# One unit earlier for x: loading, normalising and turning an x tile in three successive units, and eight products of zeros at the start

## The chip, the cores and the metric

The kernel runs on one core of a Trainium2 chip. The metric is the device time of one execution in microseconds (us). TensorE is called PE, VectorE DVE, ScalarE ACT, GpSimd POOL, SyncE SP. All transfers of this part of the kernel are issued on SP's queue, in the order of the program.

## The reference

A cross-attention layer and a feed-forward layer with a shared and sixteen routed experts, on x of 32 sequences by 100 tokens by 512. All is f32.

```
x = x + xattn(layernorm(x), ctx, ctx, WQ, WK, WV, Wfc, bfc)
      # 16 heads of 32; q = ln(x) WQ^T, k = ctx WK^T, v = ctx WV^T, causal softmax(q k^T / sqrt(32)) v
x = x + ffn(layernorm(x))
      # shared gated FFN over all tokens, and 16 experts that each take their 12 best tokens of a sequence
```

With the causal mask only the first 100 rows of a context are ever attended to. The change touches only the first layernorm, the one ahead of q, and the start of the program.

## The kernel before, in words

**Products.** A product that needs f32 accuracy is made of three: each operand is split into a high part (rounded to fp32r by a copy on ACT) and a low part (the rest, a subtraction on DVE or POOL). `mm3` (L55) issues the three for each of four slices of 128. Plain f32 products are used where operands are small: the scores, the values and all turns.

**Stages.** The attention works on 8 super-blocks of 4 sequences (400 tokens), numbered sb. A super-block has 4 units, one for each group of 4 heads, c = 0 to 3; u = 4 sb + c counts the 32 units. Around them:

- A *prologue* loads and splits WK, WV and WQ, projects the first blocks of the context to keys (kproj, L55, kept by kkeep, L200, and stored to kD, L201) and values (vproj, vkeep), and makes the four x tiles of super-block 0.
- A *unit* u computes the scores of unit u-1 (L236 into the tile sc), its row maximum (sm_max, L247, 16 instructions on DVE), subtracts it (sm_sub, L256, POOL), takes the exponential (sm_exp, L260, ACT), the row sum (sm_sum, L265, DVE) and multiplies with its reciprocal (sm_mul, L271, POOL), each in two halves. For unit u-2 it turns the four probability tiles (p_turn, L277, kept on ACT by p_keep, L282) and multiplies them with the values (values, L292, kept a unit later by y_keep, L299). It projects the query of unit u (qproj, qkeep L226) and, in the units up to 28, a piece of a later block of the context: always a kproj, and a vproj except where ck reaches the block's number of 128-row pieces, which is so in all units with c = 0 from unit 4 on.
- *x tiles.* An x tile is one sequence, 100 by 512. x_load (L145) fetches it, x_stats (L152, L153 on DVE, L154, L155 on POOL) takes mean and 1/sqrt(var), x_norm (L161, DVE, in place) normalises, x_turn (L167) turns its four slices on PE and splits the result into xnh (ACT, L100) and xnl (DVE, L101). In unit u the tile number c of super-block sb+1 has its statistics, its norm and its turn, all in this unit; its load is issued at the start of the unit before.
- The *feed-forward* part follows. It is not touched.

**Order.** The order on each engine is written out by hand (`manual_schedule`): every engine takes its instructions in program order, so the place of a call in the unit is its place in each queue that it uses. Within a unit the calls that matter here stand so:

```
kload, ctx_load, x_load | scores, y_keep, sm_max/sm_sub x2, qproj/qkeep, sm_exp(0)
p_turn(0,1), p_keep | x_stats | sm_exp(1), sm_sum(0), sm_mul(0) | kproj/kkeep
p_turn(2,3), p_keep | x_norm | sm_sum(1), sm_mul(1) | ctx_split | vproj/vkeep | x_turn | values
```

In units 9 to 12 a piece of Wfc is split as well (fc_split, L573 and L574), and unit 13 loads and prepares constants of the feed-forward part (load_consts, L563 to L569).

**Buffers.** The accumulators in PSUM are few: two tiles of `kv` (shared by kproj, vproj and qproj), two of `ms` (p_turn, values, x_turn) and one of `sc`. An instruction that writes a tile waits until the one before in that tile has been emptied. x has 5 buffers.

## Time and profile before

| | us |
|---|---|
| median of 3 runs | 1734.94 (1734.51 to 1736.95) |
| the profiled execution | 1736.99, of which the span of instructions is 1735.2 |
| PE busy | 1698.0 |
| DVE / ACT / POOL busy | 900.6 / 692.2 / 442.3 |
| prologue | 0 to about 41 |
| units | about 41 to 385 |
| feed-forward | the rest |
| one unit with a vproj, without | about 10.7, about 9.8 |

A row of the profile's timeline gives start, duration, engine, line, operation, the tiles written and read, and the count of instructions merged in the row; in brackets stands how long the engine was idle before it and what released it. A row of the list of waits gives who waited for whom, the sum, the number of times and the longest. A row of the table by windows gives the stretch, its length, the busy time of PE, of PE's weight loads, DVE, ACT and POOL with the number of instructions, then PE's granted clock (1.00 is full), the DMA engines' share and GB/s.

### The profile page before, as it was taken

The numbers are of one execution on the slowest core, as the hardware profiler recorded it, in microseconds if no ns is written. First come the engines' busy times: TensorE is split into PE (matmuls) and PEld (weight loads), VectorE is DVE, ScalarE is ACT, GpSimd is POOL, SyncE is SP. The second block draws the span as 40 slices with busy tenths as digits, with TensorE's granted clock in tenths as the row PEclk, the third lists the DMA queues.
The fourth block names the chain that finished last, engine by engine and source line by source line (L and its number), as shares of the span: only waits on it lengthen the run. The fifth ranks groups of instructions, "written<-read, shape, count | busy, mean of one in ns | idle before, by whom it ended". The sixth has DMA issues, their size and how long they took to land.

```text
span 1735.2 us, 28064 instructions
## 1 busy us (share of the span) xinstructions
PE 1698.0 (98%) x11072; PEld 1559.9 (90%) x11072; DVE 900.6 (52%) x2126; ACT 692.2 (40%) x1094; POOL 442.3 (25%) x399
## 2 busy tenths in 40 slices
PE   7999999989999999999999999999999999999999
PEld 6888888878899999998899999999999999999998
DVE  4877777785333433344654444544444454444442
ACT  4555555544221111122344444444444444444442
POOL 3777777661110110210111111111111111111011
PEclk9999999989999999999999999999999999999999
DMA  6445443434210211130445554555554554554452
GB/s 203 147 138 152 137 132 118 134 109 159 91 62 13 73 61 52 59 110 31 156 159 153 154 155 147 155 154 146 164 151 144 161 156 136 164 164 119 137 170 61
DMA packets 86836, 220.58 MB, mean 127 GB/s; under 512 B 9745, under 2 KB 38146, under 8 KB 86704
## 3 DMA queue, kind: packets, MB, share of 16 engines
q1 hardware_dynamic: 75632, 193.30, 34.1%
q0 software_dynamic: 10784, 25.21, 7.8%
q8 instruction: 87, 1.43, 0.4%
q14 instruction: 45, 0.37, 0.1%
q10 hardware_dynamic: 288, 0.27, 0.0%
HBM read 171.57 MB, written 47.18 MB: 126 GB/s over the span
## 4 chain that ended last, share of the span: by engine, by line
PE 93%; DVE 2%; POOL 2%; DMA 1%; ACT 1%; issue 1%; SPq 0%; ACTq 0%; POOLq 0%; DVEq 0%
PE gu L55 47%; PE dn L55 23%; PE kv L55 10%; PE m L55 4%; PE ms L277 2%; PE sc L236 2%; PE ms L292 2%; POOL p L256 1%; PE m L803 1%; DVE p L247 1%; DVE xt L161 1%; PE ms L167 1%; DMA kD<-kk 1%; PE m L918 1%; PE m L909 1%
## 5 line engine op out<-in xcount | busy, mean ns | idle before, releaser
L55 PE MATMUL gu<-xh,whl 128*128 128x384 f32 (+1 forms) x3200 | 645.1, 333 | 1.3 <-ACT g L655 1.3
L55 PEld LDWEIGHTS gu<-xh,whl 128*128 128x128 f32 x3200 | 558.9, 188 | 18.7 <-ACT g L655 1.5
L628 DVE TENSOR_TENSOR whl<-wraw,whl 128x1536 fp32r<-128x1536 f32 (+1 forms) x146 | 256.1, 1754 | 253.5 <-ACT whl L627 253.4
L55 PE MATMUL dn<-whl,hh 128*128 128x512 f32 x1168 | 372.2, 400 | 0.0
L55 PE MATMUL gu<-xl,whl 128*128 128x384 f32 (+1 forms) x1600 | 338.1, 333 | 0.0
L55 PEld LDWEIGHTS gu<-xl,whl 128*128 128x128 f32 x1600 | 280.6, 188 | 0.0
L659 ACT CAST hh<-g 128x384 fp32r<-128x384 f32 (+1 forms) x200 | 100.9, 505 | 431.5 <-DVE g L656 431.5
L656 DVE TENSOR_TENSOR g<-g,gu 128x384 f32<-128x384 f32 (+1 forms) x200 | 108.7, 543 | 295.5 <-PE gu L55 294.5
L627 ACT CAST whl<-wraw 128x1536 fp32r<-128x1536 f32 (+1 forms) x146 | 213.2, 1460 | 109.9 <-PE dn L55 108.9
L55 PEld LDWEIGHTS dn<-whl,hh 128*128 128x128 f32 x1168 | 213.0, 189 | 37.2
L55 PE MATMUL dn<-whl,hl 128*128 128x512 f32 x584 | 230.9, 395 | 0.0
L655 ACT ACTIVATE g<-gu 128x384 f32<-128x384 f32 (+1 forms) x200 | 96.8, 484 | 294.8 <-PE gu L55 294.7
L817 POOL DMA_INDIRECT out_dram<-x,isl x48 | 77.7, 1619 | 368.2 <-ACT x L816 358.4
L660 DVE TENSOR_TENSOR hl<-g,hh 128x384 fp32r<-128x384 f32 (+1 forms) x200 | 112.1, 560 | 114.3 <-ACT hh L659 114.3
L792 POOL DMA_INDIRECT big<-xnD,isl x48 | 49.2, 1025 | 412.3 <-PE m L803 345.6
L55 PEld LDWEIGHTS dn<-whl,hl 128*128 128x128 f32 x584 | 109.8, 188 | 26.1
L271 POOL TENSOR_TENSOR p<-p,sm 100x800 f32<-100x800 f32 x64 | 101.3, 1583 | 52.3 <-DVE sm L266 39.6
L256 POOL TENSOR_TENSOR p<-p,mx 100x800 f32<-100x800 f32 x64 | 96.5, 1529 | 49.4 <-DVE mx L247 49.4
L247 DVE CUSTOM_DVE_ANT_0 p<-sc,mask 100x100 f32<-100x100 f32 x512 | 95.6, 257 | 17.4 <-PE sc L236 17.4
L861 POOL TENSOR_TENSOR x<-x,bfc 128x512 f32<-128x512 f32 x22 | 38.7, 1786 | 185.0 <-DMA x<-x 185.0
L265 DVE TENSOR_REDUCE sm<-p 100x8 f32<-100x800 f32 x64 | 62.7, 979 | 13.4 <-ACT p L260 13.3
L260 ACT ACTIVATE p<-p 100x800 f32<-100x800 f32 x64 | 56.2, 878 | 17.5 <-POOL p L256 17.5
(143 smaller groups left out, 1655.3 us busy)
## 6 DMA issues: line engine op xcount, KB each, us to landing
wraw<-wE SPq DMA_DIRECT2D x144, 768.0 KB, 4.4
xt<-x SPq DMA_DIRECT2D x32, 200.0 KB
vD<-vt SPq DMA_DIRECT2D x25, 256.0 KB, 2.0
kt<-kD SPq DMA_DIRECT2D x32, 200.0 KB, 4.5
v<-vD SPq DMA_DIRECT2D x8, 800.0 KB
xnD<-xn SPq DMA_DIRECT2D x25, 256.0 KB, 2.0
out_dram<-x SPq DMA_DIRECT2D x25, 256.0 KB, 2.0
yD<-y SPq DMA_DIRECT2D x31, 200.0 KB, 4.4
```

The lines of the kernel that those rows point to most:

```text
L55: r = nc.tensor.matmul(out, t[0][a], t[1][b], start=(first and i == 0), stop=(last and i == n - 1))
L247: nc.vector.tensor_tensor_reduce(out=p[:, bb, h, :], in0=sc[:, h, cs], in1=mask, scale=ISCALE, scalar=NEG, op0=ALU.add, op1=ALU.max, accum ...
L256: nc.gpsimd.tensor_tensor(pv, pv, mx[:, :, None].to_broadcast([S, 8, S]), ALU.subtract)
L265: nc.vector.tensor_reduce(sm, pv, AX.X, ALU.add)
L271: nc.gpsimd.tensor_tensor(pv, pv, sm[:, :, None].to_broadcast([S, 8, S]), ALU.mult)
L627: nc.scalar.copy(h[:, cs], r[:, cs])
L628: nc.vector.tensor_tensor(l[:, cs], r[:, cs], f32(h[:, cs]), ALU.subtract)
L655: nc.scalar.activation(g[:, 0:t], pg[:, 0:t], AF.Gelu)
L656: nc.vector.tensor_tensor(g[:, 0:t], g[:, 0:t], pu[:, 0:t], ALU.mult)
L659: nc.scalar.copy(hh[:, 0:t], g[:, 0:t])
L660: nc.vector.tensor_tensor(hl[:, 0:t], g[:, 0:t], f32(hh[:, 0:t]), ALU.subtract)
L817: ins = nc.gpsimd.indirect_dma_start(out=self.K.out, out_offset=bass.IndirectOffsetOnAxis(ap=r.isl[:, i:i + 1], axis=0), in_=o, in_offset= ...
```

## The change

Three things are done.

1. The unit that turns tile (sb+1, c) no longer takes its statistics and its norm: unit u takes those of the tile that unit u+1 turns, and loads the one after that. The prologue takes over the first load, statistics and norm. x_norm stands behind sm_mul(1) now instead of ahead of sm_sum(1). The tiles xnh and xnl are taken at x_turn instead of at x_load.
2. Where a unit has no vproj, x_turn writes to a `kv` tile instead of an `ms` tile.
3. At the start of the prologue, PE multiplies a tile of zeros with itself eight times (128 by 128, f32), into an `ms` tile that nobody reads.

```diff
+WARM = 8
         def x_load(sb, b):
-            if b == 0:
-                cur["xh", sb] = xnp[sb % 2].tile([128, NC4, SB], FR, name="xnh")
-                cur["xl", sb] = xnp[sb % 2].tile([128, NC4, SB], FR, name="xnl")
             xt = xp.tile([S, D], F32, name="xt")
...
-        def x_turn(sb, b):
+        def x_turn(sb, b, own=True):
+            if b == 0:
+                cur["xh", sb] = xnp[sb % 2].tile([128, NC4, SB], FR, name="xnh")
+                cur["xl", sb] = xnp[sb % 2].tile([128, NC4, SB], FR, name="xnl")
             xt = cur["x", sb, b]
-            tp = ps_ms.tile([128, NC4, 128], F32, name="ms")
+            if own:
+                tp = ps_ms.tile([128, NC4, 128], F32, name="ms")
+            else:
+                tp = ps_kv.tile([128, D], F32, name="kv").rearrange("p (c t) -> p c t", c=NC4)
...
             nc.gpsimd.dma_start(mask, K.mask)
+            z = stp.tile([128, 128], F32, name="zero")
+            nc.vector.memset(z, 0.0)
+            zp = ps_ms.tile([128, NC4, 128], F32, name="ms")
+            for _ in range(WARM):
+                nc.tensor.matmul(zp[:, 0, :], z, z, start=True, stop=True)
...
+            x_load(1, 1)
             ctx_load(3, 0)
+            x_stats(1, 0)
             vkeep(1, 0, vproj(1, 0))
+            x_norm(1, 0)
...
+                xn = divmod(u + 5, NC4) if u + 5 < NU else None
...
-                    sn, bn = divmod(u + 5, NC4)
+                    sn, bn = divmod(u + 6, NC4)
                     if sn < nsb:
                         x_load(sn, bn)
...
-                if xs:
-                    x_stats(sb + 1, c)
+                if xn:
+                    x_stats(*xn)
...
-                if xs:
-                    x_norm(sb + 1, c)
                 if a is not None:
                     sm_sum(a, 1)
                     sm_mul(a, 1)
+                if xn:
+                    x_norm(*xn)
...
                 if xs:
-                    x_turn(sb + 1, c)
+                    x_turn(sb + 1, c, vv)
```

## The prediction

> **What bounds the kernel now.** I read the shares of busy time first, then the list of who waited for whom, then single units in the timeline, then TensorE's busy time and granted clock in windows.

> ```profile
> PE 1698.0 (98%) x11072; PEld 1559.9 (90%) x11072; DVE 900.6 (52%) x2126; ACT 692.2 (40%) x1094; POOL 442.3 (25%) x399
> ```

> TensorE (PE) is busy 98% of 1735.2 us, so 37 us are idle, and little but those can be won. "Busy" however says nothing of the clock at which it is busy. The list of waits tells who holds the idle time:

> ```profile
> PE ms L167 <- DVE xt L161: 10.4, 7, 1.7
> PE kv L55 <- ACT cxh L134: 4.9, 1, 4.9
> PE ms L277 <- ACT pt L282: 4.1, 3, 2.2
> ```

> The largest entry is x_turn (L167) waiting for x_norm (L161): 10.4 us in 7 waits. There are 28 such turns in the units; only 7 wait. Six of them are in units 4, 8, 12, 16, 20, 24, where no vproj stands between the last p_turn and x_turn (1.64 to 1.67 each), and one in unit 1 (0.46). Unit 4, in the timelines of the four engines:

> ```profile
> 78.79 0.85 PE L277 MATMUL ms<-ident,p 100*100 100x100 f32 x8
> 81.28 0.54 PE L167 MATMUL ms<-ident,xt 100*128 100x100 f32 x4 [1.64 <-DVE xt L161]
> 81.74 0.89 PE L292 MATMUL ms<-pt,v 100*32 100x100 f32 x32
> 79.38 1.75 DVE L161 TENSOR_SCALAR xt<-xt,mv,rs 100x512 f32<-100x512 f32 x1 [0.20 <-POOL rs L155]
> 79.33 1.52 POOL L271 TENSOR_TENSOR p<-p,sm 100x800 f32<-100x800 f32 x1
> 79.72 0.91 ACT L282 COPY pt<-ms 100x400 f32<-100x400 f32 x2
> ```

> x_norm takes 1.75 us here, 0.50 where POOL is idle (fastest of its 32): it runs beside sm_mul on POOL. From p_turn to values (L292) go 81.74-78.79 = 2.95 us. Unit 28 is the same unit with no x tile in it:

> ```profile
> 338.50 0.85 PE L277 MATMUL ms<-ident,p 100*100 100x100 f32 x8
> 339.99 0.89 PE L292 MATMUL ms<-pt,v 100*32 100x100 f32 x32 [0.64 <-ACT pt L282]
> ```

> There it is 1.49 us, set by ACT's copies of pt. That is the floor for the other six.

> The clock shows a second cost. Each row is a stretch of 3.4 us: busy times by engine, granted clock:

> ```profile
> 79.93:83.35 3.42, 2.07 (x68) 1.83 (x68) 2.87 (x4) 2.10 (x5) 1.86 (x2) 1.00 0.67 203
> 83.35:86.80 3.45, 3.45 (x31) 3.29 (x25) 3.20 (x33) 0.50 (x1) 3.08 (x4) 1.00 0.26 96
> 120.90:124.30 3.40, 1.73 (x37) 1.44 (x39) 3.11 (x5) 2.59 (x6) 1.97 (x2) 0.98 0.40 107
> 124.30:127.70 3.40, 3.40 (x54) 2.93 (x45) 1.64 (x12) 0.55 (x2) 2.48 (x2) 0.51 0.81 262
> ```

> Unit 8's wait lies wholly in one stretch (busy 1.73 of 3.4), and the next runs at half clock. Unit 4's wait is cut by a boundary (2.07 busy), and the clock stays. Units 12, 16 and 20 are like unit 8 (1.84, 1.74, 1.98 busy, then 0.51 to 0.52), unit 24 like unit 4. From values to the next p_turn it is 4.02 us in unit 4 (85.76-81.74) and 5.53 in unit 8 (129.29-123.76): a half-clock stretch costs 1.5 us.

> [...] here 1.98 us busy or less was enough and 2.07 was not; I use the measured bound. [...]

> **The change part by part.**

> 1. *x_norm leaves the unit of its x_turn.* x_stats and x_norm now serve the tile turned one unit later; the counts stay (28 of each, one now in the prologue). In units 4, 8, 16, 20 and 24 x_turn follows p_turn at once: p_turn 0.64 + x_turn 0.46 = 1.10 us, then values waits 0.39 for pt until the floor of 1.49. x_turn's result goes to a kv buffer there, last emptied by qkeep 3 us earlier, so the second ms buffer stays free for values. Saved: 2.95-1.49 = 1.46 each, **7.3 us** in five units.

> 2. *Half-clock stretches.* 0.39 us idle leaves about 3.0 busy, above the bound of 2.07. Those after units 8, 16 and 20 go: 3 x 1.52 = **4.6 us**.

> 3. *Unit 12 pays nothing.* In unit 13, load_consts makes ACT copy gw after a DMA:

> ```profile
> 172.15 0.25 ACT L568 CAST gw<-gr 128x64 fp32r<-128x64 f32 x1 [4.23 <-DMA gr<-gwT]
> 177.12 0.94 PE L277 MATMUL ms<-ident,p 100*100 100x100 f32 x8 [1.29 <-ACT pt L282]
> ```

> DVE's sm_max stands behind gw, then POOL, ACT's exp and pt, then PE at 177.12. That DMA is issued behind unit 12's kk store at 165.45, which x_turn does not move. So PE comes 1.46+1.54 earlier and waits 4.3 instead of 1.29. Gain 0; 4.3 us idle throttles a window of its own: I take a **loss of 1.2** (0 to 1.7).

> 4. *Unit 1:* its wait of 0.46 goes, but x_norm(1,1) now runs in unit 0 ahead of xnl and of sm_max(0), which starts some 0.9 us later (x_stats 0.9, rs 0.9, x_norm up to 1.3 in a stretch where DVE was idle from 41.4 to 42.9). Net **+0.2** (-0.5 to +0.46).

> 5. *DVE at the end of the unit:* x_norm now follows sm_sum(1). From unit 4: exp(1) ends 79.48, reduce 1.01, reciprocal 0.12, so x_norm asks at 80.6, when sm_mul(0) ends (80.8) and before sm_mul(1) can start (reciprocal to sm_mul is 0.35, so 80.9). [...] done at 81.3, xnl at 82.1, just when the next sm_max is due (scores at 81.1 + 1.03). Cost 0, hidden by the way to scores. If x_norm loses to sm_mul(1) it ends near 82.6, xnl 83.1, sm_max is 0.9 late, and p_turn(2) of the next unit, with 0.4 us of slack behind pt (88.13 to 88.56), waits 0.5. In units with vproj DVE stands idle 1.2 us before xnl, which covers it.

> 6. *SP, POOL, tiles.* One x load (200 KB) goes ahead of a ctx load in the prologue, each later one a unit earlier; 5 buffers hold the 3 tiles alive, and that ctx tile is split a unit later: 0. POOL's pairs of rs keep their places but for one ahead of cxl(2,3), 1.3 us later, needed by kproj at 45.98 against 43.4: 0.

> 7. *Eight products of zeros.* No such row exists. Sixteen f32 products of sc take 0.89 us four side by side, so one of N=100 is 0.22, of N=128 0.28 at full clock, 0.57 at half: eight take 2.3 to 4.5 us. PE is empty until 4.87; after a memset behind DVE's at 0.80 they start at about 1.0 and end at 3.3 to 5.5, at most 0.6 late. The early products may then run at 0.12 instead of 0.21 us apart, but PE stands still from 14.5 to 17.42 anyway (first line: the chain of waits, second: ACT's timeline):

> ```profile
> 9.59 7.31 DMA kD<-kk
> 17.00 0.37 ACT L200 COPY kk<-kv 128x256 f32<-128x256 f32 x1 [3.36 <-DMA kD<-kk]
> ```

> The store is issued behind a weight load that waits for DVE (9.10), so neither side reaches it. **0**; from -0.3 to +1.0, if a longer pause moves half clock past 22.72, where PE becomes the bound.

> Sum: 7.3+4.6+0.2-1.2 = 10.9 us, against the profiled execution: 1736.99-10.9 = **1726.1**. The median before is 1734.94, 2.1 below it: about one half-clock stretch less, I suppose. As the change takes such stretches out, I put the changed kernel's median at **1726**, 0.5% faster. The end of attention (370 to 384 at half clock) can move by a stretch or two either way: +-3.

> **The rivals.** [...] point 5's second case. Against it: x_norm asks first; for it: in unit 0 x_norm started at 40.04, POOL's cxl at 40.08, and x_norm still took 1.33. Five times 0.5 less, and unit 2 waits too: about 1729. *Idle moves (0.10):* the long wait in unit 13 throttles two windows, the attention's end gets one more, and part of the pt wait grows: gain near 4, 1731 to 1733. *The zeros are too late or do nothing:* within point 7. *Slower (0.05):* [...] It ends at 83.8, xnl at 84.3, sm_max is 2.2 late, p_turn(2) waits 1.8 in place of 1.46 saved, and 1.8 idle throttles as now: 5 x 0.35 + 1.2 + 1 = 4 us slower, 1739. It decides once sm_max is over 1.86 late. Against it: POOL's queued pieces let a waiting DVE in at 461 us, where yl took 2.02 us between bias pieces.

> **How the numbers follow.** Forecast 0.63, with its rivals as above. 0.2% (3.5 us) is about what a measurement can tell here. Faster: the first two and a share of the third, 0.88; same 0.07; slower 0.05. Range: 1722.5 (two stretches less at the end) to 1731.5 [...].

> **What would show it.** Right: no wait of L167 on xt; values 1.5 us after p_turn in units 4 to 24; no half clock between 50 and 165 us; a wait of some 4 us in unit 13; L161 near 0.6 us. Wrong: L277 waiting 0.5 us or more for pt after each such unit, or half-clock stretches that stay; or a first kD store issued later than 9.6.

## The result, and the profile after

| | before | after |
|---|---|---|
| median, us | 1734.74 (4 runs, 1734.51 to 1736.95) | 1722.50 (4 runs, 1720.68 to 1723.04) |
| the profiled execution, us | 1736.99 | 1723.04 |
| its span, us | 1735.2 | 1721.3 |

The ratio after to before is 0.9925, with an interval of 0.9908 to 0.9942: 0.75% faster. The profiled executions lie 13.95 us apart. The forecast was 1726 and 10.9 us between the profiled executions; 1722.5 is the lower edge of its range. So the direction and the mechanism are to be confirmed, and 3 us are to be found that the sum did not have. The profiled execution before is a slow one of its kind: 28 later runs of the kernel before took 1732.08 to 1737.33 us, with a median of 1734.19.

The first part of the page, the line of busy times. TensorE (PE) stays the bound:

```profile
PE 1692.7 (98%) x11088; PEld 1555.8 (90%) x11088; DVE 872.7 (51%) x2127; ACT 690.5 (40%) x1094; POOL 445.8 (26%) x399
```

Idle time of PE falls from 37.2 to 28.6 us (1721.3-1692.7). Busy time falls too, by 5.3 us, although sixteen instructions on zeros have been added: the same work is done at a higher clock (the mean granted clock is 0.994, after 0.990 before). Both halves of the gain are visible in one line.

PE's list of waits (who waited for whom, sum, times, longest):

```profile
PE kv L56 <- ACT kk L204: 4.8, 2, 3.1
PE ms L281 <- ACT pt L286: 3.9, 4, 2.2
PE ms L922 <- ACT pt L286: 3.5, 2, 3.2
PE ms L296 <- ACT pt L286: 3.2, 8, 0.7
PE ms L281 <- ACT y L303: 2.0, 1, 2.0
```

The entry of 10.4 us at the head of the list before, x_turn waiting for x_norm, is gone (x_turn is L171 now, p_turn L281, values L296, p_keep's pt L286). New are six waits of values for pt (3.2 us in 8, where there were 1.4 in 2) and one of 2.0 us of a p_turn for y.

Unit 4 in the timelines of PE, DVE, ACT and POOL:

```profile
78.09 0.85 PE L281 MATMUL ms<-ident,p 100*100 100x100 f32 x8
78.78 0.51 PE L171 MATMUL kv<-ident,xt 100*128 100x100 f32 x4
79.57 0.89 PE L296 MATMUL ms<-pt,v 100*32 100x100 f32 x32 [0.29 <-ACT pt L286]
79.93 0.50 DVE L159 TENSOR_SCALAR xt<-xt,mv,rs 100x512 f32<-100x512 f32 x1
80.75 0.57 DVE L102 TENSOR_TENSOR xnl<-kv,xnh 128x400 fp32r<-128x400 f32 x1 [0.32 <-ACT xnh L101]
79.01 0.91 ACT L286 COPY pt<-ms 100x400 f32<-100x400 f32 x2
78.62 3.19 POOL L275 TENSOR_TENSOR p<-p,sm 100x800 f32<-100x800 f32 x2
```

x_turn follows p_turn without a gap. From p_turn to values it is 79.57-78.09 = 1.48 us (2.95 before, 1.49 forecast), and ACT's copies of pt set it, as in unit 28. x_norm takes 0.50 us about the seam between the two sm_mul of the POOL row, and the two together take 3.19 us, 0.15 more than twice the 1.52 that one of them took before. The group of x_norm in the table by line gives minimum, median and maximum in ns of its 32 executions; the median before was 1752:

```profile
L159 DVE TENSOR_SCALAR xt<-xt,mv,rs x32: 494/497/1217, 19.5 to 305.8; 100x512 f32<-100x512 f32 x32
```

The table by windows (busy us of PE, its weight loads, DVE, ACT, POOL; then PE's granted clock) shows the stretch with the end of unit 8 and the one behind it, then two of unit 13, then two of unit 29:

```profile
118.20:121.60 3.40, 3.07 (x76) 2.68 (x78) 2.70 (x6) 3.40 (x8) 3.30 (x5) 1.00 0.30 84
121.60:125.00 3.40, 3.40 (x37) 3.25 (x30) 3.30 (x34) 0.56 (x2) 3.07 (x3) 1.00 0.87 270
164.70:168.10 3.40, 1.38 (x12) 1.18 (x11) 1.32 (x14) 1.03 (x3) 0.00 (x0) 0.99 0.17 46
168.10:171.50 3.40, 3.22 (x12) 2.71 (x10) 3.04 (x23) 1.34 (x3) 2.90 (x2) 0.51 0.17 58
331.90:335.30 3.40, 1.35 (x11) 1.30 (x12) 1.86 (x2) 3.27 (x6) 2.82 (x3) 1.00 1.04 370
335.30:338.70 3.40, 3.40 (x9) 2.63 (x9) 3.33 (x6) 1.48 (x4) 1.56 (x2) 0.50 0.98 383
```

Unit 8 has 3.07 busy of 3.40 (1.73 before), and the next stretch keeps the full clock (0.51 before). In unit 13 and in unit 29 a half-clock stretch remains.

**Where the time came from.** The lead of a unit is the start of its scores in the trace before less that in the trace after. Its growth, place by place:

| place | forecast, us | lead from ... to ... | measured, us |
|---|---|---|---|
| prologue | 0 | 0 to -0.03 | -0.03 |
| units 1 to 3 | +0.2 | -0.03 to 0.71 | +0.7 |
| units 4 and 24, the wait | 2.9 | 0.71 to 2.17; 11.62 to 13.08 | 2.9 |
| units 8, 16, 20, wait and half clock | 9.0 | 2.16 to 5.21; 5.65 to 8.65; 8.64 to 11.62 | 9.0 |
| units 12 and 13 | -1.2 | 5.21 to 5.66 | +0.45 |
| units 29 to 31 | 0 | 13.08 to 13.00 | -0.1 |
| from scores of unit 32 to the end | 0 | 13.00 to 13.94 | +0.9 |
| sum | 10.9 | | 13.9 |

The body of the forecast, 11.9 us from five units, was measured to a tenth. Three small entries were wrong, and all three in the same direction: units 12 and 13 by 1.65 us, units 1 to 3 by 0.5, the end of attention (the last two rows) by 0.8.

### The profile page after: what moved, and what is told of

It reads as the page before. It is cut to its first block, busy times and chain, and to the rows that moved or that the text cites. A ratio compares the mean times of both kernels' runs of the same rounds, so it can differ in the third digit from the quotient of the medians.

```text
span 1721.3 us, 28098 instructions
## 1 busy us (share of the span) xinstructions
PE 1692.7 (98%) x11088; PEld 1555.8 (90%) x11088; DVE 872.7 (51%) x2127; ACT 690.5 (40%) x1094; POOL 445.8 (26%) x399
## 4 chain that ended last, share of the span: by engine, by line
PE 93%; DVE 2%; ACT 2%; DMA 1%; POOL 1%; issue 1%; SPq 0%; ACTq 0%; POOLq 0%; DVEq 0%
PE gu L56 47%; PE dn L56 24%; PE kv L56 10%; PE m L56 4%; PE ms L281 2%; PE sc L240 2%; PE ms L296 1%; PE m L816 1%; POOL p L260 1%; DVE p L251 1%; ACT pt L286 1%; DMA kD<-kk 1%; PE m L931 1%; PE m L922 1%; PE ms L171 0%
## 5 line engine op out<-in xcount | busy, mean ns | idle before, releaser
L56 PEld LDWEIGHTS dn<-whl,hh 128*128 128x128 f32 x1168 | 213.1, 189 | 37.2
```

Of the source, the lines that this page charges most:

```text
L56: r = nc.tensor.matmul(out, t[0][a], t[1][b], start=(first and i == 0), stop=(last and i == n - 1))
```

## The experiments

Each median is compared with runs of the kernel before on the same chip in the same series; the medians before were 1734.19 (e0, e1, e2, e7), 1733.65 (e3 to e6) and 1733.94 (e8 to e10).

### The change once more

No edit.

> The changed kernel itself, timed once more beside the others of this series: 1722 to 1723 us, 0.9925 of the kernel before. Half-clock stretches are expected at other places than in the first profile [...], but none behind units 4, 8, 16, 20 and 24.

Measured: 1723.45 us (1722.67 to 1724.30), ratio 0.9938 (0.9924 to 0.9951). The gain between medians is 10.7 us here and 12.2 in the first series: both more than the 8.9 that the forecast left after its last step. In this execution no half-clock stretch lies between 22.2 and 356.7 us, so even the one in unit 13 is not always there; at attention's end one of 17.1 us is. The lead grows place by place as in the first profile, by 0.43 us over units 12 and 13 among others.

### The zeros taken out, and the zeros alone

e1 takes them out of the kernel after; e2 puts them into the kernel before:

```diff
-            z = stp.tile([128, 128], F32, name="zero")
-            nc.vector.memset(z, 0.0)
-            zp = ps_ms.tile([128, NC4, 128], F32, name="ms")
-            for _ in range(WARM):
-                nc.tensor.matmul(zp[:, 0, :], z, z, start=True, stop=True)
```

> The changed kernel without the eight products of zeros. My theory (the zeros are worth nothing: until 16 us the products wait for the first store of kD, and what they win is lost again before the units start): 1722.5, and the turn of the first tile of unit 0 still at 41.7 us. Rival (the zeros brought the 1.3 us by which PE restarted earlier, 16.09 against 17.42 us): 1723.8, PE restarting at 17.4.

> The kernel before with the eight products of zeros alone. My theory: 1734.7, no difference. Rival: 1.3 us less, 1733.4, PE restarting at about 16.1 us.

Measured: e1 1722.64 us, ratio 0.9938 (0.9924 to 0.9952), the same ratio as e0 with them. e2 1735.67 us, ratio 1.0006 (1.0000 to 1.0013). The zeros gain nothing, with and without the rest of the change; the interval of e2 leaves room for a loss of some 2 us, not for a gain. How they come to nothing is seen in PE's timeline of the kernel after:

```profile
1.08 3.52 PE L316 MATMUL ms<-zero 128*128 128x128 f32 x16 [1.08 <-DVE zero L313]
5.08 0.39 PE L56 MATMUL kv<-cxh,wh 128*128 128x256 f32 x1 [0.48 <-ACT cxh L135]
16.09 0.50 PE L56 MATMUL kv<-wh,cxh 128*128 128x512 f32 x1 [3.07 <-ACT kk L204]
```

Eight products, recorded as sixteen instructions, take 3.52 us (2.3 to 4.5 forecast) and end before the first operand is there. The projections behind them do run faster: their products take 0.28 us each from about 7 us on, where the kernel before has 0.41 until 11.5. The traces of e3, e4, e6 and e9, which have the zeros, show 0.28 from about 7 us as well; that of e7, which starts without them, shows 0.41 until about 11. In the execution of the kernel after, PE then restarts after the kD store at 16.09 us instead of 17.42; a later wait and a half-clock stretch from 21.3 to 24.7 take it all back (lead -0.03 at the first scores). Over the executions that were profiled, the lead at the first scores lies between -0.14 and 1.28 us in kernels with the zeros and between -0.01 and 0.80 in kernels without: the spread is not the zeros'. What the shorter products win ends at a store: PE stands still from 13 to 16 us, waiting for it, and again for 1.72 us up to 21.20, with half clock behind.

### Zeros in the gap, everything else as before

To tell half clock from wait: e7 leaves x_norm and x_turn where they were in the kernel before, and fills the wait ahead of x_turn in units 4, 8, 12, 16, 20 and 24 with products that nobody reads.

```diff
                     vkeep(j, ck, vproj(j, ck))
+                if xs and c == 0 and u > 0:
+                    zp = ps_kv.tile([128, D], F32, name="kv")
+                    for _ in range(6):
+                        nc.tensor.matmul(zp[:, 0:128], K.zero, K.zero, start=True, stop=True)
                 if xs:
```

> The kernel before, with six products of zeros (f32, 128x128, into a kv tile that nobody reads) on PE ahead of x_turn in units 4, 8, 12, 16, 20 and 24, where PE otherwise stands idle for 1.66 us; six take about 1.3 us, so they fit the gap and move nothing by themselves. Theory (the gap itself trips half clock in the window that holds it): no half-clock stretch behind these units, 1.5 us saved for each one that the kernel before has there (three to four count, as unit 12's is absorbed by the wait in unit 13): 1729 to 1731. Rival (half clock has another cause, or filling delays x_turn): 1734.7 or slower.

Measured: 1729.90 us (1729.00 to 1731.66), ratio 0.9975 (0.9964 to 0.9985): 4.3 us faster with six times six products more. PE's timeline in unit 8:

```profile
120.78 0.85 PE L277 MATMUL ms<-ident,p 100*100 100x100 f32 x8
121.46 1.53 PE L487 MATMUL kv<-zero 128*128 128x128 f32 x12
123.30 0.53 PE L167 MATMUL ms<-ident,xt 100*128 100x100 f32 x4 [0.31 <-DVE xt L161]
123.76 0.89 PE L292 MATMUL ms<-pt,v 100*32 100x100 f32 x32
127.78 0.85 PE L277 MATMUL ms<-ident,p 100*100 100x100 f32 x8
```

x_turn comes no earlier after p_turn than before (2.52 us, where the kernel before has 2.51 in this unit), so the time of the wait is all there. But from values to the next p_turn it is 127.78-123.76 = 4.02 us, where the kernel before took 5.53, and no half clock follows. The lead against the kernel before grows by 1.5 us in each of units 8, 16 and 20, by 0.6 in unit 12 and 13, and by nothing in units 4 and 24. So the second term of the sum is a cost of its own, and the smaller gain at unit 12 is the wait in unit 13 taking what comes to it. The two terms side by side, in units 4, 8, 12, 16, 20 and 24 of the traces (start to start, us):

| kernel | p_turn to values | values to the next p_turn |
|---|---|---|
| before | 2.95 to 2.98 | 4.0 in units 4 and 24, 5.5 in the other four |
| e7, the wait filled | 2.95 to 2.98 | 4.0 in all six |
| after | 1.48 to 1.52 | 4.0 in all six |

### x_turn in an ms tile again

```diff
-                    x_turn(sb + 1, c, vv)
+                    x_turn(sb + 1, c)
```

> The changed kernel with x_turn always in an ms tile. Theory: in units 4 to 24 x_turn waits for the first pt copy (1.49 us behind p_turn) and values stand 1.95 us behind p_turn instead of 1.49, so 0.46 is lost in each of five units: 1724.8. Rival (x_turn's tile makes no difference, values wait for pt anyhow): 1722.5.

Measured: 1723.64 us (1723.28 to 1726.01), ratio 0.9947 (0.9934 to 0.9961). PE's timeline in unit 4:

```profile
77.80 0.85 PE L281 MATMUL ms<-ident,p 100*100 100x100 f32 x8
79.28 0.56 PE L171 MATMUL ms<-ident,xt 100*128 100x100 f32 x4 [0.64 <-ACT pt L286]
79.78 0.89 PE L296 MATMUL ms<-pt,v 100*32 100x100 f32 x32
```

x_turn now waits until p_turn's tile is copied out, and from p_turn to values it is 1.98 us instead of 1.48 (1.95 was forecast). Five times 0.5 is 2.5 us, and from unit 4 to unit 29 the lead indeed grows by 9.8 us against 12.4. The median does not show it: from the scores of unit 32 to the end this execution took 1355.6 us and the kernel after 1357.6, for the same program. The price of the tile is shown in the trace; in the time it is smaller than what the end of attention varies by.

### x_norm ahead of sm_sum(1) again, still a unit early

```diff
+                if xn:
+                    x_norm(*xn)
                 if a is not None:
                     sm_sum(a, 1)
                     sm_mul(a, 1)
-                if xn:
-                    x_norm(*xn)
```

> The changed kernel with x_norm ahead of sm_sum(1) again (for the tile of the next unit). Theory (x_norm then starts just behind sm_mul(0) [...]): L159 takes 1.75 us again, DVE is busy some 28 us more, xnl ends about 0.8 us after the next sm_max is due, and the p_turn(2) of units 5, 9, 17, 21, 25 waits up to 0.4: 1722.5 to 1724.5. Rival (x_norm's place decides the gain, as the 1.75 us come back on the path): 1727 or more.

Measured: 1726.25 us (1726.01 to 1727.85), ratio 0.9958 (0.9944 to 0.9972), 2.8 us above e0 and between the two cases expected. x_norm, sm_mul and the next unit's two p_turns in the timelines:

```profile
79.19 1.75 DVE L159 TENSOR_SCALAR xt<-xt,mv,rs 100x512 f32<-100x512 f32 x1 [0.20 <-POOL rs L153]
79.14 1.52 POOL L275 TENSOR_TENSOR p<-p,sm 100x800 f32<-100x800 f32 x1
82.22 1.52 POOL L275 TENSOR_TENSOR p<-p,sm 100x800 f32<-100x800 f32 x1 [1.56 <-DVE sm L270]
84.67 3.00 POOL L260 TENSOR_TENSOR p<-p,mx 100x800 f32<-100x800 f32 x2
87.54 0.94 PE L281 MATMUL ms<-ident,p 100*100 100x100 f32 x8 [0.46 <-ACT pt L286]
```

x_norm takes 1.75 us again. It holds up sm_sum(1) behind it on DVE, and so sm_mul(1), which starts at 82.22. ctx_split and then the next unit's sm_sub stand behind it on POOL, and at the end of this row of queues p_turn(2) waits for pt. Unit 5 takes 0.7 us longer, as do four others, and unit 2 waits 1.02. The expectation allowed up to 0.4 per unit; with POOL's queue in the chain it is more. So the place behind sm_mul(1), which the forecast booked at nothing, is what keeps the early norm free: with x_norm a unit early and in its old place 4.3 us of the lead at unit 29 are lost (8.74 against 13.08).

### The constants loaded two units earlier

e5 in the kernel before, e6 in the kernel after: the three loads of load_consts are issued in unit 11, and only gw's preparation stays in unit 13.

```diff
-                if u == FC_AT + NC4:
+                if u == FC_AT + 2:
                     F.load_consts()
+                if u == FC_AT + NC4:
+                    F.prepare_consts()
...
+    def prepare_consts(self):
+        nc, gw, gr = self.nc, self.gw, self.gr
         nc.scalar.copy(gw[:, :, 0:NE], gr)
```

> The kernel before with load_consts' loads and memset in unit 11 instead of 13, and the copy and subtraction of gw in unit 13 as before. Theory: the wait of 1.29 us in unit 13 goes and no more: 1733.4. Rival (the DMA of gr isn't what unit 13 waits for): 1734.7.

> The changed kernel with the same edit. Theory (unit 12's gain was absorbed by the wait for gr in unit 13): that wait, 4 us of delay between the two pairs of p_turn in unit 13, shrinks to some 1.2 (wfl still makes sm_max late), so 2.8 us are saved, more than twice what the same edit saves in the kernel before: 1719.7. Rival: the same 1.3 as in the kernel before, 1721.2.

Measured: e5 1732.04 us (1729.39 to 1734.41), ratio 0.9990 (0.9982 to 0.9999), 1.6 us less than before. e6 1719.18 us (1718.31 to 1720.00), ratio 0.9914 (0.9899 to 0.9929), 4.3 us less than e0 and 3.3 less than the first series of the change. In the traces unit 13, from scores to scores, shortens from 13.8 to 12.3 us in the kernel before and from 14.8 to 12.2 in the kernel after: the same edit is worth 1.5 us there without the change and 2.6 with it (1.3 and 2.8 expected). The medians go the same way, but they come from different series and their intervals are too wide for a factor. From unit 13 to unit 14 the lead grows from 7.52 to 9.11 in e6, and falls from 6.66 to 5.66 in the kernel after. What is left of the wait, in e6's timeline of PE:

```profile
168.01 0.95 PE L281 MATMUL ms<-ident,p 100*100 100x100 f32 x8 [1.21 <-ACT pt L286]
```

This is the absorption of the prediction's point 3, measured by taking the absorber away: in the kernel after, what unit 12 gains is held back in unit 13 until gr has landed.

### The rest of unit 13's wait

e8 moves gw's preparation on to unit 14, and the last piece of Wfc from unit 12 to unit 13.

```diff
+FCU = [9, 10, 11, 13]
...
-                if FC_AT <= u < FC_AT + NC4:
-                    fr = load_w(3, u - FC_AT)
+                if u in FCU:
+                    fr = load_w(3, FCU.index(u))
...
+                if u == FC_AT + NC4 + 1:
+                    F.prepare_consts()
```

> The changed kernel with load_consts' loads and memset in unit 11, gw's copy and subtraction in unit 14, and the last piece of Wfc loaded and split in unit 13 instead of 12 (so that DVE's wfl no longer stands between x_norm and xnl in a unit without vproj). Theory (unit 13's wait had two causes, the DMA of gr and then wfl): unit 13 takes 10.75 us from scores to scores, as units 5 and 9 do, where the run with the early constants alone needed 12.21: 1.4 us less than that run, 1717.8. Rival (what was left had another cause): 1719.

Measured: 1719.27 us (1717.92 to 1720.01), ratio 0.9911 (0.9898 to 0.9925). Unit 13 takes 10.77 us in the trace, as an undisturbed unit does and as expected, but the median is that of e6 and not the 1717.8 expected; the five runs spread over 2.1 us, more than the 1.4 in question.

### The end of attention filled, and all together

e9 puts eight products of zeros into unit 29's gap and twelve into unit 31's (`fill(n)` is n products of zeros into a `kv` tile that nobody reads); e10 is e8 and e9 together.

```diff
                 if end == 2:
+                    fill(12)
                     pr.turn(0)
...
+                if end == 0:
+                    fill(8)
                 if back is not None:
```

> The changed kernel with products of zeros on PE in two gaps at the attention's end: eight ahead of the second pair of p_turn in unit 29 (gap 2.15 us, eight take 1.8 at full clock) and twelve ahead of the first turn of the feed-forward part in unit 31 (gap 3.2 to 3.7, twelve take 2.6). Theory (the spread of the runs, and up to 3 us of the time, is half clock behind these gaps, 7 to 17 us long in the runs so far): at most one half-clock stretch between 330 and 385 us, 2 to 4 us saved against the changed kernel, 1718.5 to 1720.5, with less spread. Rival (the end of attention is bound by ACT and POOL, so PE's clock there is worth nothing): 1722.5 to 1723.5; if the products are still running at half clock when pt comes, slower.

> Both of the above together, the version to beat the others: the two gains add up if they are independent, 1717.8 - 3 = about 1715. If the half clock at the end is worth nothing, 1717.8.

Measured: e9 1721.82 us (1720.78 to 1722.14), ratio 0.9925 (0.9912 to 0.9939); e10 1718.46 us (1715.52 to 1720.48), ratio 0.9905 (0.9889 to 0.9921). PE's timeline of e9 in unit 31:

```profile
353.65 2.87 PE L314 MATMUL kv<-zero 128*128 128x128 f32 x24
357.52 0.66 PE L930 MATMUL ms<-ident,xn 128*128 128x128 f32 x4 [1.00 <-ACT pt L287]
359.67 0.55 PE L282 MATMUL ms<-ident,p 100*100 100x100 f32 x4 [1.14 <-ACT pt L287]
```

After the gaps the clock stays full (one half-clock stretch, at 379.6, where the kernel after has three from 335 us on), but PE still waits for ACT's pt: between 320 and 390 us 4.9 us in all, where the kernel after has 8.5. Against e0 the gain is 1.6 us, against the first series 0.7, less than the 2 to 4 expected: the clock comes back and brings little. What else bounds this end was not settled. e10 has the lowest median of all, 4 to 5 us under the change, above the 1715 expected and not clear of e6 and e8.

## Why the prediction was right or wrong, point by point

- **What bounds the kernel: right.** The idle time behind the six turns was 10.4 us on the list of waits, and it was what could be won, with the half clock on top.
- **1, the wait: right.** 1.46 to 1.47 us in each of five units. The floor was read from unit 28, a unit without the step, and the changed units stand on it to 0.03 us. e3 shows that the `kv` tile is half a microsecond of this.
- **2, the half clock: right.** 1.5 us each behind units 8, 16 and 20. e7 shows it as a cost separate from the wait.
- **3, unit 12 pays nothing: the wait right, the loss of 1.2 wrong. This is the step that failed.** A loss of 1.2 us was taken for a half-clock stretch of unit 13's own; 0.45 was gained, and these 1.65 us are more than half of the 3.05 that the sum lacks. The wait and the half clock came as forecast. In the timelines of ACT and PE of the kernel after:

```profile
166.50 0.24 ACT L581 CAST gw<-gr 128x64 fp32r<-128x64 f32 x1 [4.18 <-DMA gr<-gwT]
170.94 0.87 ACT L286 COPY pt<-ms 100x400 f32<-100x400 f32 x2
168.52 1.49 PE L56 MATMUL kv<-cxl,wh 128*128 128x384 f32 x4
171.46 0.94 PE L281 MATMUL ms<-ident,p 100*100 100x100 f32 x8 [0.18 <-ACT pt L286]
```

  The 4 us of waiting are now split. y_keep stands behind gw on ACT, and the first half of p_turn waits 2.02 us for it ahead of kproj; kproj then runs at half clock (1.49 us for four) and ends just as pt is ready, so p_turn waits only 0.18. The half clock fell on work that had slack, and cost nothing. From gw to that p_turn it is 4.96 us after and 4.97 before: its start is set by gr alone. e0 shows the same without the stretch: there kproj runs at full clock, p_turn waits 1.59 us, and it still comes 4.96 us behind gw. The prediction knew that p_turn had to wait there, and still charged 1.2 us for the stretch. The 0.45 gained is gr landing 6.26 us after the issue of unit 12's kk store instead of 6.70. In the nine profiled executions that load gr in unit 13 this lies between 6.00 and 6.96, with and without the change, so the sign of the 0.45 is chance: over units 12 and 13, e0, e1 and e9 gain 0.43, -0.03 and -0.39. A loss of 1.2 came in none of them. Why the landing varies is open.
- **4, unit 1: too small,** +0.7 instead of +0.2. Two things were mis-sized. sm_max(0) was only 0.54 us later, at 43.89, and nothing waited for it. And the wait of 0.46 is counted from the modelled end of the product before it; from the start of vproj's last four products to x_turn it was 1.53 us (49.23 to 50.76) and is 0.92 (49.26 to 50.18), so 0.61 was to be won. The last tenth was not followed up.
- **5, DVE at the end of the unit: the forecast case,** x_norm at 0.50 us. The cost is 0. That x_norm would come between the two sm_mul was an estimate. The traces show its duration, 1.75 us where sm_mul starts 0.05 us ahead of it (unit 4 before, and e4) and 0.50 us here, 1.31 us behind the start of the first sm_mul; what sets it they do not show. That this was worth a point is shown by e4, where 0.7 us go in each such unit.
- **6 and 7: right.** No wait for an x load appears: in the trace DVE never stands idle ahead of x_stats. And the zeros are worth nothing (e1, e2).
- **The end of attention:** held in the range by 3 us either way, and booked at 0. In the first profile, unit 29's wait of 2.2 us for pt was there before, cut by a window's boundary (2.20 busy in one, 2.47 in the next); shifted by 13 us it falls into one window (1.35 busy) and costs a stretch. In return there is less half clock behind unit 31: two windows on end from 359.2, where four ran on end from 370.1 before. Net +0.8 over the two last rows of the table. Which windows trip there differs from execution to execution of the same kernel (e0 has 17.1 us on end and none at unit 29), so this part is chance.
- **The last step held; the sum ahead of it was short.** From 1726.1 for the profiled execution the text went to 1726 for the median, 2.05 us less gain than the sum, because the profiled execution before seemed to have one half-clock stretch more than a median run, which the change would take out. The profiled executions came 13.95 us apart and the first medians 12.24: 1.7 less. The reason given fits as well, though nothing tests it alone: the profiled execution before had a mean granted clock of 0.990, while 25 of the 28 runs beside e0 had 0.991 to 0.993, and there those with 0.991 took 1735.7 us on average, those with 0.992 took 1733.3. So the 3.5 us between 1726 and 1722.5 are the 3.05 of the sum and 0.4 of this step. Which units trip differs: in the profiled execution before 8, 12, 16 and 20; with the zeros (e2) or with the constants moved (e5), 4, 12, 16 and 24, or 4, 12 and 20.

**The rivals.** The second case of point 5 did not come: no p_turn waits 0.5 us for pt behind these units. *Idle moves* came in two of its three parts, a half-clock stretch in unit 13 and one in unit 29; the first cost nothing, and the second was given back. *Slower* did not come; e4 is as near to it as a run got, and is still 0.4% faster than before. That *the zeros do nothing* is so.

## What to carry to other kernels

When an engine waits whose clock falls after a wait, as PE's fell here behind all 31 windows with at most 1.50 of 3.41 us busy, charge the wait and the clock apart, and look at which work the slow stretch will fall on: on work with slack, as kproj in unit 13 (1.49 us for four, and p_turn still 4.96 us behind gw), it cost nothing. Before putting an operation a step earlier, follow every queue behind its new place, here DVE's and then POOL's, since the place was worth as much as the step. And see where the execution that a sum is made from lies among the other runs: here it was a slow one, and 1.7 us of its gain do not show in the medians.

## What the runs showed of the hardware that was not expected

```profile
366.70:370.10 3.40, 0.65 (x8) 0.44 (x6) 3.29 (x33) 0.84 (x2) 1.91 (x2) 0.98 0.00 0
370.10:373.50 3.40, 1.81 (x9) 1.48 (x9) 1.87 (x4) 3.16 (x6) 3.32 (x4) 0.50 0.20 77
373.50:376.90 3.40, 3.40 (x44) 2.78 (x48) 2.97 (x5) 1.61 (x4) 1.73 (x2) 0.50 0.00 0
376.90:380.40 3.50, 3.44 (x44) 2.96 (x40) 3.05 (x25) 1.36 (x3) 0.33 (x1) 0.50 0.17 61
380.40:383.80 3.40, 3.40 (x43) 2.59 (x41) 1.61 (x13) 2.24 (x5) 2.68 (x2) 0.53 0.02 5
383.80:387.20 3.40, 3.40 (x24) 3.12 (x21) 2.50 (x5) 2.36 (x6) 1.53 (x1) 1.00 0.16 60
```

  PE is busy throughout from 373.5 and yet stays at half clock for three windows more. So the busy time of the profile alone does not tell when the clock comes back; these windows are full of turns, scores and values, and whether that is the reason was not tried. Such a stretch took 6.8 to 17.1 us in those executions that have one, and from the scores of unit 32 to the end the thirteen executions took 1355.6 to 1358.6 us: a spread as large as what e3 and e9 change.
- **Products of zeros can pay.** In each of six units of e7 six of them filled a wait (twelve records, 1.53 us in unit 8), and together they were worth 4.3 us in the time, by the clock of what came after.
